# Block attention with a residual layer norm: softmax weights moved into the values' copy, the last row in halves, and a new order

## The chip, the cores and the metric

The kernel runs on one NeuronCore of a Trainium2 chip. Such a core has five engines with queues of their own: TensorE (PE in the profile, with its weight loads as PEld), VectorE (DVE), ScalarE (ACT), GpSimd (POOL) and SyncE (SP), which here only issues transfers. The metric is the device time of one execution in microseconds. Before the change it is 143.77 us, the median of three runs (143.69, 143.77, 144.44).

## The reference, cut to what matters

The input `x` is [8, 512, 1024] in float32. Each of the 8 batches is cut into 8 blocks of 64 rows, which are summed; the block sums are projected to keys, normalized, scored against one query, and a softmax over the 8 blocks weights the block sums. The weighted sum is projected by `Wo` to one vector for the batch, which is added to every row; the rows are then layer-normalized and added to `x`:

```python
block_repr = inputs.reshape(B, n_blocks, block_size, H).sum(axis=2)
keys = jnp.einsum('bnh,kh->bnk', block_repr, Wk)
keys = keys / rms * rms_weight
attn = jax.nn.softmax(jnp.einsum('bnh,h->bn', keys, q), axis=-1)
attended = jnp.einsum('bn,bnh->bh', attn, block_repr)      # the same for all rows of a batch
x = inputs + jnp.einsum('bsh,kh->bsk', attended, Wo)
out = (x - mu) / jnp.sqrt(var + EPS) * ln_gamma + ln_beta
return inputs + out                                        # 8 x 512 x 1024
```

The kernel uses that with y = inputs + proj the result is y * (1 + gamma * rs) + (beta - proj - mean * gamma * rs), where rs is one over the deviation: one multiplication of the row by a vector, and one addition of a vector, both different for every row.

## The kernel before, in words

The 4096 rows of `x` are worked in four groups of two batches (`GROUPS`). A group is 4 tiles `x_0` to `x_3` of 128 partitions with two rows each, so 8 rows of 1024 elements on every partition, and 32 such rows, k = 0 to 31, in all. Two successive rows are a unit (`UNITS`), 16 in all.

Before the first group both weight matrices are loaded, transposed on TensorE (L427) and copied to `wkT` and `woT` (L434), by VectorE for the copies in `EV_DVE` and else by ScalarE. The first 7 loads are three tiles of `Wk` and the four tiles of group 0; then come the last of `Wk`, `Wo`, and the `x` tiles of the other groups. There are 13 tile buffers (`XBUFS`), so later tiles wait for a weight tile to be transposed or for a store.

Each group goes through these steps:

- TensorE sums the blocks, `bs` (L592, four tiles); VectorE transposes the sums, `blkT` (L605); TensorE projects the keys (L460; L485 in group 0).
- ScalarE and VectorE take the squares and the product with the query (L624, L628); TensorE spreads them to all partitions, `pc` (L637, L640); ScalarE and VectorE make the scores and the softmax (L644 to L669). The result is `own`, one weight for each partition, where a partition stands for one block and one quarter of the columns.
- TensorE projects the values (L460, 32 steps of four narrow matmuls), ScalarE copies them to `val` (L700). Two selection matrices are scaled by `own` on ScalarE: `w` (L675) and `pickw` (L679).
- TensorE spreads the projected vector to all partitions, `pb` (L706), from `val` and `w`. It also makes the table `ptab` (L713, L714) from `val` and `pickw`, and from the matrix `gb`, which holds gamma and beta, with `pickv`. ScalarE copies it to `tab` (L718). The table holds, for each batch, the vectors that `b` needs.

Each row then goes through these:

- y (L759): VectorE adds `pb` to the row and sums it.
- Squares (L767): ScalarE takes the sum of the squared deviations, `ssq`.
- For a unit: GpSimd adds epsilon to `ssq` (L812), raises it to the power -0.5, `rs` (L813), and writes the row's factors to `stat` (L817, L822). TensorE transposes them, `pl` (L827), and ScalarE (for the units in `LT_ACT`) or VectorE copies them, `lt` (L834).
- Multiplication: for 26 rows ScalarE makes 1 + gamma * rs, `A` (L861), and GpSimd multiplies the row by it, called v here (L866). For the 6 rows in `ON_DVE` and `ON_BOTH` TensorE makes the factor in PSUM, `pA` (L872, L851), and VectorE multiplies (L878).
- Addition: TensorE makes the vectors to be added of both rows of the unit, `b` (L895), and VectorE adds them (L908), called out here. Then SP stores the tile (L915), the rows of the last two tiles one by one (L921).

The buffers that couple these steps are few. The two rows' banks of `b` are one pair, so the next `b` starts when both additions of the unit before are done. `stat` is one tile. `A` has three buffers, `lt` two. The bank `s2` is shared by values, `ptab` and `pl`.

The order of all this is written out. Every step is registered with `plan.add(engine, cost, emit, needs, ...)` and gets a number; `ORDER` lists the numbers in the order in which the instructions are emitted, and so fixes the order on each engine's queue. `FILLS` puts filler matmuls (`e_fill`, L952) ahead of a step: products of the identity with `gam` into a part of a bank that nobody reads. A filler leaves two records of 0.38 us that overlap; four fillers in a row took 1.89 us together.

Of the kernel before, what the change touches and what calls it, by code (L numbers as in the profile page):

```python
# [37 lines left out]
LT_ACT = (2, 3, 4, 5, 6, 7, 8, 9, 10, 11, 12, 13, 14, 15)  # L38
# [8 lines left out]
EV_DVE = (2, 3, 6, 9, 12, 15)  # L47
Y_PARTS = ()
EARLY_SUMS = 2
ROW_STORES = 2  # L50
ORDER = (
    0, 12, 1, 5, 6, 2, 3, 4, 7, 8, 9, 11, 10, 22, 24, 13, 63, 14, 25, 15, 26, 30, 27, 16, 23, 32,
    31, 55, 54, 28, 33, 17, 64, 29, 18, 57, 56, 65, 19, 20, 21, 66, 67, 70, 86, 34, 71, 68, 35, 36,
    69, 37, 58, 40, 38, 72, 73, 39, 42, 74, 41, 44, 75, 43, 76, 87, 48, 78, 77, 88, 46, 45, 79, 47,
    60, 59, 89, 49, 80, 81, 50, 90, 61, 52, 82, 51, 83, 91, 85, 53, 84, 95, 92, 93, 96, 94, 97, 98,
    173, 103, 99, 105, 104, 107, 106, 109, 174, 101, 102, 100, 119, 108, 175, 111, 120, 121, 125,
    176, 122, 113, 123, 110, 126, 127, 177, 115, 178, 179, 114, 117, 133, 180, 134, 129, 124, 135,
    181, 139, 137, 136, 191, 183, 182, 140, 128, 118, 184, 192, 130, 185, 131, 62, 116, 141, 186,
    138, 193, 187, 112, 194, 188, 143, 160, 142, 189, 267, 195, 147, 166, 198, 144, 145, 161, 190,
    162, 199, 268, 163, 148, 164, 167, 201, 149, 269, 150, 200, 203, 151, 165, 202, 205, 270, 146,  # L60
    204, 152, 153, 132, 196, 215, 206, 216, 271, 221, 154, 228, 207, 197, 222, 272, 155, 232, 273,
    156, 219, 234, 217, 274, 229, 233, 209, 157, 158, 168, 218, 211, 208, 230, 275, 170, 235, 231,
    285, 276, 169, 210, 286, 277, 213, 171, 220, 172, 223, 212, 159, 278, 225, 214, 287, 241, 224,
    279, 288, 254, 245, 280, 226, 227, 236, 242, 289, 246, 281, 243, 282, 237, 361, 283, 247, 255,
    292, 238, 258, 248, 362, 293, 239, 240, 260, 363, 295, 244, 294, 259, 364, 297, 249, 296, 365,
    299, 366, 298, 309, 256, 261, 367, 257, 300, 250, 251, 368, 313, 369, 301, 252, 253, 310, 322,
# [95 lines left out]
def block_attn_resid_kernel(  # L162
# [14 lines left out]
    HALF = 512  # L177
    QU = H // 4
    RT = 2
    UNIT = 4  # L180
    FAR = 1e30
    RS = float(H) ** 1.5
    assert RS == 2.0**15
# [267 lines left out]
    def project(rank, lhs, wT, tag, name, needs, hold, end, takes=None, parts=4):  # L451

        i = None
        for c0 in range(0, HC, HC // parts):
            def emit(c0=c0):
                if c0 == 0:
                    hold["po"] = half_bank(tag, name)
# [529 lines left out]
```

## Time and profile before

| | us |
|---|---|
| median of three runs | 143.77 |
| the profiled execution, whole | 144.35 |
| its span, first to last instruction | 142.6 |
| TensorE busy | 123.2 |
| VectorE busy | 100.0 |
| ScalarE busy | 95.2 |
| GpSimd busy | 84.2 |
| mean granted TensorE clock | 0.922 of full speed |

The profiled execution took 0.58 us more than the median, and 1.75 us of it lie outside the span. Durations below are from this one execution. The duration of an instruction is longer than the distance to the next on the same engine, because instructions overlap: y lasts 1.21 us, and the next starts 1.14 us after it. The distance is what counts on a full queue. The slices of busy time have one digit for each fortieth of the span, 3.57 us, in tenths. Where a row ends in brackets, the engine stood idle before it for that time, and the name is what it had waited for.

The stages show in the rows of instructions: the first y starts at 45.29 us, that of group 1 at 65.11, of group 2 at 88.21 and of group 3 at 109.74. The last addition on VectorE ends at 138.87.

### The profile page before, as it was taken

The page shows a single profiled execution, that of the slowest core. Times are in us where ns is not written, and L with a number is a line of the kernel's source. Part 1 is how long each engine was busy: PE and PEld are TensorE (multiplying, and loading weights), DVE is VectorE, ACT ScalarE, POOL GpSimd, SP SyncE. Part 2 cuts the span into 40 slices and gives each one's busy share as a digit, 9 for nine tenths or more (in the row PEclk, how much of TensorE's full clock was granted, in tenths as well). Part 3 has the DMA queues.
Part 4 walks back from the last instruction along what each step waited for, and adds up shares of the span by engine and source line. Part 5 has one row for each costly group of instructions (what it writes and reads, how often), then busy time and mean ns, then how long its engine had stood idle before and what let it go on. Part 6 is the DMA issues. An engine that isn't in the chain of part 4 may idle for free.

```text
span 142.6 us, 3107 instructions
## 1 busy us (share of the span) xinstructions
PE 123.2 (86%) x1202; PEld 68.8 (48%) x1202; DVE 100.0 (70%) x172; ACT 95.2 (67%) x165; POOL 84.2 (59%) x103
## 2 busy tenths in 40 slices
PE   0398996999999999999999999999898597799940
PEld 0375952875875745544544545446344264233400
DVE  6203121331462998687999989999999999986790
ACT  0306521345761999989999888998997999946000
POOL 7200000000020159998999999999989999999700
PEclk9999999999999999999999999999999959855555
DMA  4999999999999980199985499907616606756285
GB/s 114 428 403 426 418 408 406 409 414 423 416 423 414 420 365 21 74 310 414 375 292 241 184 306 379 379 11 294 257 74 280 276 37 262 294 221 257 110 349 239
DMA packets 7118, 42.15 MB, mean 296 GB/s; under 512 B 688, under 2 KB 704, under 8 KB 3264
## 3 DMA queue, kind: packets, MB, share of 16 engines
q1 hardware_dynamic: 7072, 41.95, 73.7%
q8 instruction: 9, 0.15, 0.4%
q14 instruction: 5, 0.04, 0.1%
q10 hardware_dynamic: 32, 0.02, 0.0%
HBM read 25.18 MB, written 16.78 MB: 294 GB/s over the span
## 4 chain that ended last, share of the span: by engine, by line
PE 45%; DVE 17%; DMA 14%; POOL 7%; issue 7%; ACT 6%; DVEq 1%; ACTq 0%; POOLq 0%
DMA x<-in_x_dram 10%; DVE x L908 7%; PE pt L427 7%; DVE x L759 7%; PE b L895 7%; PE bs L592 6%; POOL x L866 5%; PE pA L872 5%; PE keys L460 4%; DMA gb<-n_L_cond_rms_weight_dram 4%; PE keys L485 3%; PE values L460 3%; PE values L485 3%; ACT sq L767 3%; PE pl L827 2%
## 5 line engine op out<-in xcount | busy, mean ns | idle before, releaser
L866 POOL TENSOR_TENSOR x<-x,A 128x1024 f32<-128x1024 f32 x26 | 61.4, 2380 | 2.0 <-ACT A L861 1.9
L759 DVE SCALAR_TENSOR_TENSOR x<-x,pb 128x1024 f32<-128x1024 f32 x32 | 37.6, 1213 | 3.9 <-PE pb L549 2.9
L767 ACT ACTIVATE sq<-x,ysum 128x1024 bf16<-128x1024 f32 x32 | 36.7, 1146 | 2.9 <-DVE x L759 2.4
L908 DVE TENSOR_TENSOR x<-x,b 128x1024 f32<-128x1024 f32 x32 | 37.7, 1216 | 1.2 <-PE b L895 0.8
L861 ACT ACTIVATE A<-gam,rs 128x1024 f32<-128x1024 f32 x26 | 29.0, 1143 | 0.9 <-POOL rs L813 0.9
L895 PE MATMUL b<-tab,lt 32*128 32x512 f32 x128 | 24.1, 724 | 1.8 <-DVE x L908 0.9
L427 PE MATMUL pt<-ident,w 128*128 128x128 f32 x128 | 18.4, 300 | 6.4 <-DMA w<-in_L_cond_Wk_dram 5.9
L525 POOL TENSOR_SCALAR pickw<-early,own 128x256 f32<-128x256 f32 x1 | 0.9, 942 | 36.3 <-DVE junk L669 36.3
L427 PEld LDWEIGHTS pt<-ident,w 128*128 128x128 f32 x128 | 16.5, 197 | 9.4 <-issue 7.9
L592 PE MATMUL bs<-x,blk 128*32 128x256 f32 x256 | 16.4, 383 | 0.8 <-DMA x<-in_x_dram 0.5
L895 PEld LDWEIGHTS b<-tab,lt 32*128 32x128 f32 x128 | 7.7, 206 | 9.4 <-issue 3.5
L813 POOL TENSOR_TENSOR rs<-ssq,power 128x2 f32<-128x2 f32 x16 | 11.3, 707 | 1.3
L460 PE MATMUL values<-woT,blkT 128*32 128x256 f32 x192 | 12.0, 382 | 0.0
L460 PE MATMUL keys<-wkT,blkT 128*32 128x256 f32 x192 | 11.8, 383 | 0.2 <-DVE blkT L605 0.2
L592 PEld LDWEIGHTS bs<-x,blk 128*32 128x32 f32 x256 | 7.2, 110 | 7.9 <-issue 2.5
L812 POOL TENSOR_SCALAR ssq<-ssq 128x2 f32<-128x2 f32 x16 | 3.6, 223 | 8.7 <-ACT sq L767 7.4
L460 PEld LDWEIGHTS values<-woT,blkT 128*32 128x32 f32 x192 | 5.6, 109 | 6.2 <-issue 2.3
L872 PE MATMUL pA<-tabf,lt 32*128 32x512 f32 x16 | 7.2, 988 | 1.6 <-DVE x L759 0.9
L878 DVE TENSOR_TENSOR x<-x,pA 128x1024 f32<-128x1024 f32 x6 | 7.2, 1218 | 1.7 <-PE pA L872 1.7
L460 PEld LDWEIGHTS keys<-wkT,blkT 128*32 128x32 f32 x192 | 5.5, 109 | 5.9 <-DVE blkT L605 2.5
L434 DVE COPY wkT<-pt 128x1024 f32<-128x1024 f32 x3 | 3.7, 1225 | 6.4 <-PE pt L427 6.4
L827 PEld LDWEIGHTS pl<-ident,stat 128*128 128x128 f32 x16 | 2.3, 144 | 10.8 <-POOL stat L817 4.2
(104 smaller groups left out, 140.3 us busy)
## 6 DMA issues: line engine op xcount, KB each, us to landing
x<-in_x_dram SPq DMA_DIRECT2D x16, 1024.0 KB, 17.2
out_dram<-x SPq DMA_DIRECT2D x14, 1024.0 KB, 4.5
w<-in_L_cond_Wk_dram SPq DMA_DIRECT2D x4, 1024.0 KB, 9.3
w<-in_L_cond_Wo_dram SPq DMA_DIRECT2D x4, 1024.0 KB, 21.2
out_dram<-x SPq DMA_DIRECT2D x4, 512.0 KB, 2.8
gb<-in_cond_dram ACTq DMA_DIRECT2D x1, 4.0 KB
gb<-n_L_cond_rms_weight_dram ACTq DMA_DIRECT2D x1, 4.0 KB
gb<-in_L_cond_ln_gamma_dram ACTq DMA_DIRECT2D x1, 4.0 KB
```

Of the source, the lines that this page charges most:

```text
L427: nc.tensor.transpose(pt[:, c, r * P : (r + 1) * P], stage[which, s][:, r, bass.ds(4 * h4 + c, P, step=HC)], ident)
L460: nc.tensor.matmul(hold["po"][32 * j : 32 * j + 32, :], lhs(c), wT[:, c, bass.ts(j, QU)], start=(c == 0), stop=(end and c == HC - 1),)
L485: nc.tensor.matmul(T["po"][32 * j : 32 * j + 32, :], columns(2 * j + c), wT[:, 2 * j + c, bass.ts(s, QU)], start=(c == 0), stop=(c == 1),)
L592: nc.tensor.matmul(T["bs"][32 * j : 32 * j + 32, :], blk[g], G["x"][t][:, r, bass.ts(j, QU)], start=(t == 0 and r == 0), stop=(t == G["til ...
L759: nc.vector.scalar_tensor_tensor(x_row(k), x_row(k), 1.0, G["pb"], ALU.mult, ALU.add, accum_out=U["sum"][:, i : i + 1])
L767: nc.scalar.activation(junk, x_row(k), AF.Square, bias=U["sum"][:, i : i + 1], scale=-float(H), accum_out=U["ssq"][:, i : i + 1],)
L813: nc.gpsimd.tensor_tensor(U["rs"][:, :N], ssq, power[:, :N], ALU.pow)
L861: nc.scalar.activation(U["A", k], gam, AF.Identity, bias=1.0, scale=U["rs"][:, k - k0 : k - k0 + 1])
L866: nc.gpsimd.tensor_tensor(x_row(k), x_row(k), U.pop(("A", k)), ALU.mult)
L872: nc.tensor.matmul(U["pA", k][:, i, :], U["lt"][lo : lo + 32, pair, :], tabf[lo : lo + 32, :], start=True, stop=True,)
L895: nc.tensor.matmul(U["b", pair][r][:, i, :], U["lt"][lo : lo + 32, pair, :], G["T"]["tab"][lo : lo + 32, :], start=True, stop=True,)
L908: nc.vector.tensor_tensor(x_row(k), x_row(k), flat(U["b", pair][k % RT]), ALU.add)
```

## The change

- `own` becomes the scale of the activation that copies the values to `val`, in groups 1 to 3. `w` and `pickw` are not made any more; the unscaled matrices `weigh` and `pick` take their places. `val` now needs `own`.
- Gamma and beta get into `val` itself: a matmul `last2` by `gb` opens the accumulation of the values and puts them in the last two rows of each quarter, `own4` makes `own` 1 there, and `pick` gets their factors. So `ptab` has two matmuls in place of four. `own4`, `last2` and the entries of `pick` are made in the setup.
- Adding epsilon is a step of its own, on ScalarE for the five units in `EPS_ACT` and on GpSimd for the others.
- Row 31, the last, is added in two halves of 512 columns, each with a store of its own.
- `ORDER` is new from the start, and so is `FILLS`: 26 fillers at 10 places instead of 5 at 2. `LT_ACT` gets unit 0, and `EV_DVE` is another choice of seven copies instead of six.
- `UNIT` is 2 instead of 4, so `stat`, `lt` and `power` are smaller, and the pool of unit sums has 8 buffers instead of 16. The lines on `Y_PARTS` change too, but `Y_PARTS` is empty and they emit nothing.

In the new order, around the places that the prediction speaks of: all four `bs` of group 1 come ahead of `ptab` of group 0. The second `b` of group 0 follows all of group 1's values instead of the first half, with one filler after it and before `pb`. On VectorE the last additions of group 0 (tile 1) still come between the softmax and the first y of group 1. On GpSimd the multiplications of the last tile of group 0 change places. In the tail the fillers stand, in this order: one before `pb` of group 3, 5 before the second `pl` after it, 8 before `ptab`, 1 before the next `pl`, 5 before unit 12's `b`, 1 before the `pA` of row 26 and 2 before that of row 28. VectorE has the same rows in the same order in the tail, and the halves of row 31 come before row 30, which is whole. On ScalarE the epsilon of unit 13 comes after the copy of the last table. SP issues 21 loads before the first store; before it were 20.

```diff
-LT_ACT = (2, 3, 4, 5, 6, 7, 8, 9, 10, 11, 12, 13, 14, 15)
+LT_ACT = (0, 2, 3, 4, 5, 6, 7, 8, 9, 10, 11, 12, 13, 14, 15)
-EV_DVE = (2, 3, 6, 9, 12, 15)
+EV_DVE = (3, 6, 7, 9, 12, 13, 14)
+EPS_ACT = (6, 7, 11, 12, 13)
...
-FILLS = {343: 1, 411: 4}
+FILLS = {200: 1, 278: 1, 292: 1, 358: 5, 390: 8, 392: 1, 412: 1, 418: 5, 428: 1, 442: 2}
...
-    UNIT = 4
+    UNIT = max(UNITS)
...
-    unit = ctx.enter_context(tc.tile_pool(name="unit", bufs=len(UNITS)))
+    unit = ctx.enter_context(tc.tile_pool(name="unit", bufs=8))
...
+        for k in range(2):
+            for row, fill in ((GAM, -RS / H), (BET, 1.0)):
+                spots(fields(pick[g], k)[:, :, :, row : row + 1], [[0, 2], [-64, 2], [0, 1]], -32 * k - row, fill)
...
+    own4 = const.tile([P, 32], F32, tag="own4", name="own4")
+    nc.vector.tensor_scalar(own4, diag4, diag4[:, GAM : GAM + 1], diag4[:, BET : BET + 1], ALU.add, ALU.add)
+    last2 = const.tile([P, P], F32, tag="last2", name="last2")
+    nc.gpsimd.memset(last2, 0.0)
+    for k in (GAM, BET):
+        nc.vector.tensor_copy(
+            last2.rearrange("p (j m) -> p j m", m=32)[:, :, k : k + 1], by[:, :, k : k + 1]
+        )
...
-                junk3, T["pc"][:, 2, :NB], T["es"], diag4[:, :NB], ALU.mult, ALU.mult, accum_out=T["own"]
+                T["pc"][:, 3, :NB], T["pc"][:, 2, :NB], T["es"], own4[:, :NB], ALU.mult, ALU.mult, accum_out=T["own"]
...
-        def e_w():
-            T["w"] = chain.tile([P, 2, P], F32, tag="w", name=f"w{n}")
-            nc.scalar.activation(flat(T["w"]), flat(weigh[g]), AF.Identity, scale=T["own"])
-
-        def e_pick():
-            T["pick"] = chain.tile([P, 2, P], F32, tag="pickw", name=f"pickw{n}")
-            nc.scalar.activation(flat(T["pick"]), flat(pick[g]), AF.Identity, scale=T["own"])
...
+        def e_vectors(po):
+
+            nc.tensor.matmul(po, last2, gb, start=True, stop=False)
...
-            nc.scalar.copy(T["val"], T["values"]["po"])
+            nc.scalar.activation(T["val"], T["values"]["po"], AF.Identity, scale=T["own"])
...
-                nc.tensor.matmul(pb[:, j, :], T["w"][v, j % 2, :], T["val"][v, :], start=True, stop=True)
+                nc.tensor.matmul(pb[:, j, :], weigh[g][v, j % 2, :], T["val"][v, :], start=True, stop=True)
...
-                nc.tensor.matmul(T["ptab"][:, k, :], T["pick"][:, k, :], T["val"], start=True, stop=False)
-                nc.tensor.matmul(T["ptab"][:, k, :], pickv[:, k, :], gb, start=False, stop=True)
+                nc.tensor.matmul(T["ptab"][:, k, :], pick[g][:, k, :], T["val"], start=True, stop=True)
...
+        def e_eps():
+
+            ssq = U["ssq"][:, :N]
+            if u in EPS_ACT:
+                nc.scalar.activation(ssq, ssq, AF.Identity, bias=epsh_t)
+            else:
+                nc.gpsimd.tensor_scalar(ssq, ssq, EPS * H**3, None, ALU.add)
...
-            nc.gpsimd.tensor_scalar(ssq, ssq, EPS * H**3, None, ALU.add)
...
+                if k == NR - 1:
+
+                    for h in range(2):
+                        def e_half(k=k, out=e_out, h=h):
+                            out(k, (NR - 1 - k0) // RT, h * HALF, h * HALF + HALF)
+
+                        halves_.append(plan.add(DVE, 0.6, e_half, [bi, v], k + R["out"]))
+                    outs.append(halves_[-1])
+                else:
+                    outs.append(plan.add(DVE, 1.14, e_out, [bi, v], k + R["out"]))
...
+                    if k == NR - 1:
+                        for h, o in enumerate(halves_):
+                            stores.append(plan.add(SP, 0.35, lambda h=h: e_store_half(h), [o], k, moved=0.25))
+                    else:
+                        stores.append(plan.add(SP, 0.35, e_store_row, [o], k, moved=0.5))
```

## The prediction

> **What bounds the kernel now.** I read the page first: the span and the slices of busy time, then the costliest groups.
>
> ```profile
> span 142.6 us, 3107 instructions
> DVE  6203121331462998687999989999999999986790
> POOL 7200000000020159998999999999989999999700
> PEclk9999999999999999999999999999999959855555
> L866 POOL TENSOR_TENSOR x<-x,A 128x1024 f32<-128x1024 f32 x26 | 61.4, 2380 | 2.0 <-ACT A L861 1.9
> L759 DVE SCALAR_TENSOR_TENSOR x<-x,pb 128x1024 f32<-128x1024 f32 x32 | 37.6, 1213 | 3.9 <-PE pb L549 2.9
> L908 DVE TENSOR_TENSOR x<-x,b 128x1024 f32<-128x1024 f32 x32 | 37.7, 1216 | 1.2 <-PE b L895 0.8
> ```
>
> From about 45 us on VectorE is full, from 56 us GpSimd too; the average shares (70%, 59%) hide that. The TensorE clock falls to half in the last fifth. To see when, the table by stretches (us, busy of PE, PEld, DVE, ACT, POOL, then granted clock, DMA):
>
> ```profile
> 112.00:114.00 2.00, 1.00 (x6) 0.56 (x3) 2.00 (x5) 2.00 (x5) 1.90 (x2) 0.90 0.51 209
> 114.00:116.00 2.00, 2.00 (x6) 1.55 (x6) 2.00 (x4) 1.94 (x5) 2.00 (x2) 0.50 0.00 0
> 116.00:118.00 2.00, 2.00 (x12) 0.87 (x10) 2.00 (x4) 1.81 (x3) 1.83 (x3) 0.75 0.31 131
> 122.00:124.00 2.00, 1.12 (x11) 0.52 (x5) 2.00 (x5) 2.00 (x5) 2.00 (x2) 0.96 1.01 422
> 124.00:126.00 2.00, 2.00 (x8) 0.88 (x8) 2.00 (x3) 2.00 (x4) 1.75 (x6) 0.50 0.25 102
> ```
>
> Half clock from 113.6 to 117.0 and from 123.8 to the end. What it costs is VectorE's timeline in the tail (start, duration, what it did, idle before):
>
> ```profile
> 125.67 1.21 DVE L878 TENSOR_TENSOR x<-x,pA 128x1024 f32<-128x1024 f32 x1
> 127.29 2.35 DVE L908 TENSOR_TENSOR x<-x,b 128x1024 f32<-128x1024 f32 x2 [0.41 <-PE b L895]
> 130.84 1.22 DVE L878 TENSOR_TENSOR x<-x,pA 128x1024 f32<-128x1024 f32 x1 [1.19 <-PE pA L872]
> 132.47 2.35 DVE L908 TENSOR_TENSOR x<-x,b 128x1024 f32<-128x1024 f32 x2 [0.41 <-PE b L895]
> 135.38 1.22 DVE L878 TENSOR_TENSOR x<-x,pA 128x1024 f32<-128x1024 f32 x1 [0.56 <-PE pA L872]
> 136.52 2.35 DVE L908 TENSOR_TENSOR x<-x,b 128x1024 f32<-128x1024 f32 x2
> ```
>
> Waits of 0.41 + 1.19 + 0.41 + 0.56 = 2.57 us, all on slow matmuls. VectorE ends at 138.87; the last store needs 3.73 more. GpSimd's last multiply ends at 134.46, so it is about 3 us from binding. Earlier, one place matters, where group 0 hands over to group 1 (TensorE, then VectorE):
>
> ```profile
> 60.13 1.14 PE L895 MATMUL b<-tab,lt 32*128 32x512 f32 x8
> 61.20 1.93 PE L460 MATMUL values<-woT,blkT 128*32 128x256 f32 x32
> 61.83 2.35 DVE L908 TENSOR_TENSOR x<-x,b 128x1024 f32<-128x1024 f32 x2
> 65.11 1.22 DVE L759 SCALAR_TENSOR_TENSOR x<-x,pb 128x1024 f32<-128x1024 f32 x1 [0.93 <-PE pb L706]
> ```
>
> TensorE works without a break from 45.2 to 65.1, and VectorE adds rows from b meanwhile.
>
> [...] here L644 (16 elements, one pointer) took 0.266.
>
> **The change, part by part**, durations from the rows of before.
>
> Scalings gone: w and pickw, 2 x 3 x 0.50 = 3.0 us of ScalarE. They do not set pb: in group 1 w ends at 62.97 and val starts at 63.20; in group 2 row sums hold TensorE until 87.03, 0.5 after w; in group 3 values end after w. The new wait of val on own queues squares and A behind it; own comes at 61.97, 85.97, 106.2, before or about when values end. [...] I take 0 (from -0.5 to +0.3).
>
> Gamma and beta: two matmuls of 0.43 fewer per ptab, one of 0.43 more per values. In groups 1 and 2 that is -0.43 each; the last ptab, 3.6 us at half clock, becomes 0.86 at full. It gates only a table needed 4 us later: 0 by itself.
>
> Epsilon on ScalarE for 5 units: GpSimd gives up 5 x 0.31 (start of L812 to start of L813) = 1.55; ScalarE takes 5 x 0.2 (an estimate from L644 less overlap), in the room of the 3.0. No trace row has this form: gain between 0 and 1.55. In unit 13 it queues behind the copy of the last table, and GpSimd's next power waits: I charge 0.2.
>
> Setup: four selects of 0.21 and two fills on GpSimd, three small operations on VectorE. Hidden: GpSimd is idle till 40.8, VectorE from 4.7 to 11.9. Unhidden it would be 1.5. The first y at 45.29 hangs on the 7th load (22.1) and an unbroken 23 us of TensorE; the 7th load is an x tile still, and the same transposes follow: 0 (+-0.3).
>
> Moved with it: one more weight copy on VectorE (1.22) and one less on ScalarE (1.02), under TensorE's 23 us; unit 0's lt from VectorE (0.2) to ScalarE (0.15); half as many buffers for the units' sums, whose last readers are eight units back; on SP the 21st load goes ahead of the first store, and the last x load still goes behind stores of group 0 (80.8, its row sums at 88 to 91, DMA about 60% busy there). All 0; a load 3 us later would stop the row sums.
>
> Halves: row 31 is added in halves, but the order puts row 30, whole, after it. So the last store stays 512 KB behind a whole addition. 128x512 has no row; between L628 (0.42 at 256) and L908 (1.22 at 1024) a half takes about 0.69, two cost 0.1 more. One more store is issued (0.33 on SP, before the last addition ends). +0.1 (from -0.3 to +0.4).
>
> The order, group 0 to 1: the second b now stands behind all of values, and one filler stands before pb. Also all four row sums come ahead of ptab, so the transpose waits about 0.5 for them. From 45.2: sums 4.0, ptab 2.8, keys 4.0, two pl 0.5, b 1.07, pc 0.8, last2 0.43, values 4.0: b starts at 62.8, ends 63.9. VectorE, through with own at 62.0, waits for it, adds two rows to 66.2 and only then starts y: 66.2 against 65.11, so **+1.05**. GpSimd is free at 66.0, but the A it takes first stands on ScalarE behind an lt, which needs the pl after pb: 67.1; twice more it waits for squares of later rows (0.6, 0.8). That is 2.4 us of gaps where before had 0.5, and the 1.55 saved pay back most of it later. Groups 1 and 2: the same rows on VectorE (65.11 to 88.21 is 23.1, 0.5 of it idle). TensorE has five row sums 5.0, keys 4.0, values with last2 4.4, four b 4.3, a pair of pA 1.1, ptab 0.9, four pl 1.0, pc 0.8, pb 1.1, two fillers 0.9: 23.5, just as full. So nothing is caught up, and I carry the 1.05 on. y of group 3 then starts at 110.8 against 109.74.
>
> The tail: the same rows on VectorE in the same order. Fillers: 5 + 8 + 1 + 5 + 1 + 2 = 22 x 0.43 (1.89 for four, less the overlap) = 9.5 us against 5 x 0.43. The stretches 110.2 to 123.8 then are over 90% busy and keep the clock. Then b (1.07) fits beside the multiplication by pA (1.13), and the **2.57 go**. What is late next: GpSimd, about 1 us later than before through the last group, makes two or three additions wait, in all 0.4 with the 0.2 above.
>
> Sum on VectorE's end: 138.87 + 1.05 + 0.1 - 2.57 + 0.4 = 137.85; plus 3.73: span 141.6 against 142.6. The profiled run took 144.35, 1.75 outside the span, and stands 0.58 above the median 143.77. With 1.75 the forecast is 143.35, by ratio to the median 142.8. I say **142.9**.
>
> **The rivals.**
> *One window lost and regained.* After 124 there are few fillers: a pA of 1.06, then about 1.1 us without work until b's bank is free. [...] Then one b, two fillers and a pA run late by 1.3 us. Span 142.9: 144.2.
> *Lost to the end* (the other side). As before, where a window full of pA and b at half clock from 123.8 did not bring it back. Two fillers then cost 1.7 us ahead of a pA, and pA with b takes 3.78 (128.64 to 132.42) in place of 2.1, in three units: VectorE ends about 3.9 later, at 141.8; span 145.5, run 146.8. It decides as soon as the clock drops before about 129.
> *GpSimd binds.* Its gaps in group 1 are larger than I walked them, or ScalarE's epsilon holds it up: 1.5 us more before it frees rows. For it: it is 95% full from 60 on. Against: 1.55 of its work is gone. Run 144.4.
> *No gain from the clock*, held but irrelevant: excluded by the idle lines above.
>
> **How the numbers follow.** The forecast 0.48 (own range 141.5 to 143.5; 0.40 of it faster, 0.08 same). One window lost 0.20 (0.12 same, 0.08 slower). Lost to the end 0.17, slower. GpSimd 0.15 (0.04 same, 0.11 slower). Faster by over 0.5% 0.40, within 0.5% 0.24, slower 0.36; 0.5% is about what a measurement of this kernel can tell from no change. A tenth lies below 140.8 (the order hides the 1.05 too); upward I go to 146.8, the case of the clock lost.
>
> **What would show it.** Right: half clock nowhere between 110 and 125; VectorE's idle from 124 on under 1 us; the first y of group 1 near 66.2 with VectorE idle before a b at 62 to 64; squares' epsilon on ScalarE near 0.2; the last store 3.7 us long. Wrong: fillers of 0.86 in the trace, a pA of 2 us, or additions waiting on GpSimd for over 2 us in all. [...]

## The result, and the profile after

| | before | after |
|---|---|---|
| median of four runs, us | 143.99 (143.69 to 144.44) | 145.48 (145.42 to 145.61) |
| profiled execution, whole | 144.35 | 145.45 |
| its span | 142.6 | 143.6 |
| first y of groups 0, 1, 2, 3 | 45.29, 65.11, 88.21, 109.74 | 45.65, 65.67, 90.02, 111.63 |
| end of VectorE's last addition | 138.87 | 139.65 |
| end of GpSimd's last multiply | 134.46 | 136.93 |

The ratio is 1.0098, with a 95% interval of 1.0069 to 1.0127: the kernel became 1% slower, where 142.9 had been forecast.

The page of the kernel after: span, slices of busy time, and the groups that answer to those shown of before.

```profile
span 143.6 us, 3196 instructions
DVE  6204001631762996849999898999999999999970
POOL 7500000000020169986869988999979997999910
PEclk9999999999999999999999999999999999999955
L884 POOL TENSOR_TENSOR x<-x,A 128x1024 f32<-128x1024 f32 x26 | 61.5, 2378 | 3.2 <-ACT A L879 3.1
L769 DVE SCALAR_TENSOR_TENSOR x<-x,pb 128x1024 f32<-128x1024 f32 x32 | 37.6, 1214 | 3.1 <-PE pb L567 2.9
L927 DVE TENSOR_TENSOR x<-x,b 128x1024 f32<-128x1024 f32 (+1 forms) x33 | 38.0, 1183 | 5.0 <-PE b L913 4.4
```

The clock row has lost its fives but for the last two. In exchange VectorE waits 5.0 us ahead of its additions, where before it was 1.2, and GpSimd 3.2 ahead of its multiplies instead of 2.0. The stretches (us, busy of PE, PEld, DVE, ACT, POOL, then clock, DMA) confirm the clock:

```profile
112.00:114.00 2.00, 2.00 (x11) 1.56 (x9) 2.00 (x5) 2.00 (x4) 2.00 (x3) 1.00 0.95 393
116.00:118.00 2.00, 2.00 (x11) 1.77 (x10) 2.00 (x4) 1.69 (x5) 2.00 (x2) 1.00 0.01 4
124.00:126.00 2.00, 1.66 (x11) 0.50 (x11) 2.00 (x5) 1.97 (x3) 2.00 (x2) 1.00 0.96 393
136.00:138.00 2.00, 1.19 (x4) 0.00 (x0) 1.43 (x3) 0.00 (x0) 0.93 (x1) 0.52 0.82 326
```

It is full to 136, where 0.50 stood before. VectorE's timeline in the tail:

```profile
127.79 1.21 DVE L896 TENSOR_TENSOR x<-x,pA 128x1024 f32<-128x1024 f32 x1
129.11 1.22 DVE L927 TENSOR_TENSOR x<-x,b 128x1024 f32<-128x1024 f32 x1
130.48 1.22 DVE L927 TENSOR_TENSOR x<-x,b 128x1024 f32<-128x1024 f32 x1
131.62 1.22 DVE L896 TENSOR_TENSOR x<-x,pA 128x1024 f32<-128x1024 f32 x1
137.23 2.42 DVE L927 TENSOR_TENSOR x<-x,b 128x512 f32<-128x512 f32 x3 [0.57 <-PE b L913]
```

The waits of 0.41, 1.19, 0.41 and 0.56 for slow matmuls are gone; 0.57 remains, for the last b, after the clock fell at 136 (its second half takes 1.61 us, from 135.58). The shorter waits between the rows, as the 1.37 from 129.11 to 130.48 in place of 1.14, are for GpSimd, whose multiplication ended at 130.44. So the tail gave about half of what it was to give: from the first y of group 3 to the last addition it takes 28.02 us, against 29.13 before and 27.05 in the forecast. The kernel is slower because group 3 starts 1.89 us later. Of that, 0.36 is there at the first y, 0.20 comes by group 1, 1.25 in group 1 itself (from 65.67 to 90.02), and 0.08 in group 2. TensorE's timeline around the places:

```profile
62.12 1.14 PE L913 MATMUL b<-tab,lt 32*128 32x512 f32 x8
63.19 0.70 PE L992 MATMUL pc<-gam,ident 128*128 128x256 f32 x2
63.82 1.14 PE L717 MATMUL pb<-val,weigh 64*128 64x256 f32 x8
...
73.00 0.70 PE L992 MATMUL bs<-gam,ident 128*128 128x256 f32 x2 [0.32 <-DVE blkT L623]
73.75 1.07 PE L478 MATMUL keys<-wkT,blkT 128*32 128x256 f32 x16
...
84.84 0.70 PE L992 MATMUL pc<-gam,ident 128*128 128x256 f32 x2 [0.21 <-ACT pc L679]
85.47 1.07 PE L478 MATMUL values<-woT,blkT 128*32 128x256 f32 x16
```

And VectorE's first y of group 2:

```profile
90.02 1.21 DVE L769 SCALAR_TENSOR_TENSOR x<-x,pb 128x1024 f32<-128x1024 f32 x1
```

L992 is a filler. Start to start, one alone takes 0.63 to 0.75 us here, not 0.43. And a filler can wait: it writes into an unread part of a bank, and the bank has other users. At 73.00 it waits 0.32 for the transposition of the row sums, as the keys behind it would (0.37 in the run without it, below), so it cannot fill that hole; at 84.84 it waits 0.21 for the softmax.

### The profile page after: what moved, and what is told of

Its sections match the earlier page's. It is cut to its first block, busy times and chain, and to the rows that moved or that the text cites. A ratio compares the mean times of both kernels' runs of the same rounds, so it can differ in the third digit from the quotient of the medians.

```text
span 143.6 us, 3196 instructions
## 1 busy us (share of the span) xinstructions
PE 126.2 (88%) x1238; PEld 71.1 (49%) x1238; DVE 101.3 (71%) x176; ACT 93.4 (65%) x164; POOL 83.7 (58%) x104
## 4 chain that ended last, share of the span: by engine, by line
PE 54%; DMA 14%; POOL 14%; DVE 8%; issue 3%; ACT 3%; DVEq 0%; POOLq 0%; ACTq 0%
DMA x<-in_x_dram 10%; POOL x L884 10%; PE b L913 8%; PE pt L443 7%; PE values L478 7%; PE keys L478 6%; PE pc L992 5%; PE bs L610 4%; DMA gb<-n_L_cond_rms_weight_dram 4%; DVE x L927 3%; PE keys L503 3%; PE values L503 3%; DVE x L769 2%; POOL rs L830 2%; DVE x L896 2%
## 5 line engine op out<-in xcount | busy, mean ns | idle before, releaser
L927 DVE TENSOR_TENSOR x<-x,b 128x1024 f32<-128x1024 f32 (+1 forms) x33 | 38.0, 1183 | 5.0 <-PE b L913 4.4
L913 PE MATMUL b<-tab,lt 32*128 32x512 f32 x128 | 21.1, 644 | 0.5 <-DVE x L927 0.2
L992 PE MATMUL pc<-gam,ident 128*128 128x256 f32 x50 | 12.7, 390 | 0.2 <-ACT pc L679 0.2
L992 PEld LDWEIGHTS pc<-gam,ident 128*128 128x128 f32 x50 | 8.9, 193 | 4.3 <-issue 2.7
L913 PEld LDWEIGHTS b<-tab,lt 32*128 32x128 f32 x128 | 6.0, 183 | 7.6 <-issue 3.1
L623 DVE STREAM_TRANSPOSE blkT<-bs 128x256 f32<-128x256 f32 x4 | 1.8, 447 | 9.8 <-PE bs L610 9.7
L824 POOL TENSOR_SCALAR ssq<-ssq 128x2 f32<-128x2 f32 x11 | 2.4, 221 | 10.0 <-ACT sq L777 9.4
L851 ACT COPY lt<-pl 128x128 f32<-128x128 f32 x15 | 3.8, 256 | 5.3 <-PE pl L844 5.2
```

What stands on the lines that cost most here:

```text
L913: nc.tensor.matmul(U["b", pair][r][:, i, :], U["lt"][lo : lo + 32, pair, :], G["T"]["tab"][lo : lo + 32, :], start=True, stop=True,)
L927: nc.vector.tensor_tensor(x_row(k)[:, c], x_row(k)[:, c], flat(U["b", pair][k % RT])[:, c], ALU.add)
L992: nc.tensor.matmul(at, ident, gam[:, :QU], start=True, stop=True)
```

## The experiments

Four theories (the first three are theories 1 to 3 of the expectations). **T1, fillers**: the four single fillers ahead of the tail are paid on TensorE's full queue. **T2, order**: the new order costs (the second b behind the values, GpSimd's gaps). **T3, parts**: val behind own, last2, and the detour of epsilon cost. **T4, clock**: the tail's fillers are worth the 2.5 us that VectorE waited. All runs, with the ratio to the kernel before on the same chip. They are from four chips, on which the medians of the kernel before lie between 143.74 and 144.00, so a difference of 0.3 us between two medians from different chips shows nothing; where a part is priced below, the marks of the profiled executions stand beside it.

| kernel | median, us | ratio, 95% interval |
|---|---|---|
| after without its four early fillers | 143.86 | 1.0009 (0.9992 to 1.0026) |
| after without any filler | 145.98 | 1.0152 (1.0126 to 1.0178) |
| all parts, old order | 146.65 | 1.0196 (1.0157 to 1.0234) |
| before, tail filled | 142.55 | 0.9914 (0.9888 to 0.9941) |
| before, tail filled, weight in val's copy only | 143.55 | 0.9970 (0.9955 to 0.9985) |
| before, tail filled, gamma and beta in the rows only | 144.21 | 1.0032 (1.0008 to 1.0055) |
| new order, old parts | 145.22 | 1.0078 (1.0050 to 1.0106) |
| all parts, old order, tail filled | 145.20 | 1.0098 (1.0055 to 1.0140) |
| after without early fillers, epsilon on GpSimd | 144.89 | 1.0070 (1.0041 to 1.0098) |
| weight in val's copy, a row sum ahead of pl | 143.02 | 0.9940 (0.9921 to 0.9960) |
| the same, five epsilons on ScalarE | 144.15 | 1.0019 (1.0008 to 1.0031) |
| before, tail filled, two early fillers | 143.66 | 0.9987 (0.9967 to 1.0008) |
| before, tail filled, row sum behind pb | 143.13 | 0.9947 (0.9928 to 0.9966) |
| after without early fillers, 3 before the table | 142.95 | 0.9942 (0.9919 to 0.9965) |

### The fillers taken away, early ones and all

```diff
-FILLS = {200: 1, 278: 1, 292: 1, 358: 5, 390: 8, 392: 1, 412: 1, 418: 5, 428: 1, 442: 2}
+FILLS = {358: 5, 390: 8, 412: 1, 418: 5, 428: 1, 442: 2}
```

> The kernel after without its four single fillers ahead of the tail (before pb of group 1, before the first quarter of group 2's keys, before the last quarter of group 2's values, before pb of group 3). Theory 1, the fillers are what the chain on TensorE pays: each stood in it for 0.63 to 0.75 us, so y of group 1 comes about 0.6 earlier (65.0), y of group 2 about 1.8 (88.2), y of group 3 about 1.8 to 2.4 (109.3 to 109.8); span 141.5 to 142.3, time 143.3 to 144.2. Theory 2, the order costs (second b of group 0 behind the values, row sums ahead of the table, gaps on GpSimd): y of group 3 comes less than 0.5 earlier and the time stays within 0.4 of the kernel after, 145.1 to 145.5.

Measured: 143.86, within what T1 gives, though only the two fillers of group 2 turn out to cost anything. The first y of the groups comes at 45.74, 65.76, 88.63 and 110.54. The filler of group 1 had cost nothing (65.67 with it, 65.76 without): VectorE was still adding its two rows while it ran. That of group 3 was covered too: without it pb waits 0.59 for val, at 109.36. The two of group 2 cost 1.39 between them (90.02 to 88.63), about what their records add up to: 0.75 + 0.63 + 0.21 of waiting, less 0.17 that a b waits when they are gone. TensorE's timeline without them:

```profile
73.09 1.07 PE L478 MATMUL keys<-wkT,blkT 128*32 128x256 f32 x16 [0.37 <-DVE blkT L623]
...
82.12 2.80 PE L478 MATMUL values<-woT,blkT 128*32 128x256 f32 x48
85.09 1.14 PE L913 MATMUL b<-tab,lt 32*128 32x512 f32 x8 [0.17 <-DVE es L684]
```

```profile
88.63 1.21 DVE L769 SCALAR_TENSOR_TENSOR x<-x,pb 128x1024 f32<-128x1024 f32 x1
```

The keys wait 0.37 for the transposition and start at 73.09; with the filler, at 73.75. Of the 1.6 us, 1.09 are there at y of group 3; the tail takes 27.56 in place of 28.02, because its last b still comes at full clock (1.00 from 134 to 136).

```diff
-FILLS = {200: 1, 278: 1, 292: 1, 358: 5, 390: 8, 392: 1, 412: 1, 418: 5, 428: 1, 442: 2}
+FILLS = {}
```

> The kernel after without any filler. If the tail's fillers are what holds the clock, it falls to half at about 112 to 114 and again near 124, VectorE's waits for pA and b from 124 on come back to about 2.5 us, and the time is 144.0 to 145.0 if the early fillers cost about 1.8 (theory 1), 146.5 to 147.5 if they cost nothing (theory 2). If the tail's fillers hold nothing, full clock stays to 136 and the time is 143 or less.

Measured: 145.98, so the tail's fillers are worth 2.12 us (145.98 against 143.86). The clock falls, as the stretches show, and from 127 on VectorE waits 0.48, 0.43, 0.60, 0.41, 0.55 and 0.42, in all 2.9:

```profile
112.00:114.00 2.00, 2.00 (x9) 0.49 (x6) 2.00 (x5) 2.00 (x5) 2.00 (x2) 0.50 0.65 262
118.00:120.00 2.00, 0.90 (x3) 0.18 (x1) 2.00 (x5) 1.87 (x4) 1.84 (x6) 0.61 0.00 0
128.00:130.00 2.00, 1.64 (x7) 0.69 (x5) 1.57 (x3) 0.50 (x2) 1.75 (x6) 0.50 1.05 438
```

The time lies between the two expectations (144.0 to 145.0, and 146.5 up). The early fillers explain 1.6 us, but this kernel without any filler is 2.2 slower than the one before, so more is lost than fillers.

### The kernel before, with its tail filled

```diff
-FILLS = {343: 1, 411: 4}
+FILLS = {343: 2, 384: 2, 411: 5, 420: 2, 424: 2, 437: 1, 451: 1}
```

> The kernel before, with fillers in its tail alone: 14 in place of 5, set before b of unit 10, the last table, b of units 12 to 15 and pA of row 26. If the half clock in the tail costs what VectorE's waits of 2.57 us show, the clock is full from 110 to 136, the waits from 124 on fall below 0.8 and the time is 141.3 to 142.5. If GpSimd or something else takes over as the bound, the clock is full and the time stays within 0.7 of the kernel before. If the fillers don't hold the clock, they cost 0.86 each and the time is 144.5 or more.

Measured: 142.55, 0.86% faster than before and 1.8% faster by ratio than after: the best of all runs. Marks up to group 3 are those of before (109.75), the clock is full past 136 (1.00 in every stretch from 108), no wait for a slow matmul is left in VectorE's timeline, and it ends at 136.85, 2.02 earlier than in the profiled execution of before. So T4 has the cause right, but not its size: 2.02, not 2.5. What is late next is GpSimd (GpSimd's timeline, then VectorE's):

```profile
129.79 4.68 POOL L866 TENSOR_TENSOR x<-x,A 128x1024 f32<-128x1024 f32 x2
```

```profile
129.50 1.22 DVE L878 TENSOR_TENSOR x<-x,pA 128x1024 f32<-128x1024 f32 x1
133.32 1.21 DVE L878 TENSOR_TENSOR x<-x,pA 128x1024 f32<-128x1024 f32 x1
134.50 2.35 DVE L908 TENSOR_TENSOR x<-x,b 128x1024 f32<-128x1024 f32 x2
```

GpSimd works with no break over 0.1 us from 124.59 to the end of its last multiplication at 134.47, and the last additions start at 134.50. VectorE's units follow each other at GpSimd's 3.82 us (129.50 to 133.32), where three of its own distances of 1.14 are 3.42. The kernel has 15 fillers (not 14, as the expectation counts): ten more than before, in places where TensorE has room, are worth 1.2 us without any of the parts.

### Parts and order: a square

The parts in the old order: each step of the kernel after was put where the old order has the same step; val took the place of w, and epsilon went right before the power.

```diff
-LT_ACT = (0, 2, 3, 4, 5, 6, 7, 8, 9, 10, 11, 12, 13, 14, 15)
+LT_ACT = (2, 3, 4, 5, 6, 7, 8, 9, 10, 11, 12, 13, 14, 15)
-EV_DVE = (3, 6, 7, 9, 12, 13, 14)
+EV_DVE = (2, 3, 6, 9, 12, 15)
-EPS_ACT = (6, 7, 11, 12, 13)
+EPS_ACT = ()
...
-FILLS = {200: 1, 278: 1, 292: 1, 358: 5, 390: 8, 392: 1, 412: 1, 418: 5, 428: 1, 442: 2}
+FILLS = {350: 1, 418: 4}
```

> All parts of the change in the code, but in the order of the kernel before, with its fillers, its choice of copies and epsilon left on GpSimd; row 31's halves stand where its whole addition stood. If the order and the fillers are what costs (theories 1 and 2), the time is that of the kernel before or a little less: 143.5 to 144.1. If the parts cost (theory 3: val behind own on ScalarE, last2 of 0.5 to 0.6 on the chain of each group), y of groups 1 to 3 comes 0.5, 1.0 and 1.5 later than before, and the time is 145 or more.

The same with its tail filled:

```diff
-FILLS = {350: 1, 418: 4}
+FILLS = {350: 2, 390: 2, 418: 5, 428: 2, 432: 2, 446: 1, 461: 1}
```

> All parts of the change in the old order as in the run before (146.65), but with the tail's fillers of the filled kernel before. The clock there fell already at 103 us, behind a stall. If most of its loss was clock, the time falls by 2 us or more, to 143.5 to 144.6; if it was the waits for val and last2 that the parts make in the old order, it falls by less than 1 us, to 145.6 to 146.5, with y of group 2 still near 90.2.

And the kernel before in the new order, with the new choices of copies:

```diff
-LT_ACT = (2, 3, 4, 5, 6, 7, 8, 9, 10, 11, 12, 13, 14, 15)
+LT_ACT = (0, 2, 3, 4, 5, 6, 7, 8, 9, 10, 11, 12, 13, 14, 15)
-EV_DVE = (2, 3, 6, 9, 12, 15)
+EV_DVE = (3, 6, 7, 9, 12, 13, 14)
...
-FILLS = {343: 1, 411: 4}
+FILLS = {350: 5, 384: 8, 405: 1, 411: 5, 420: 1, 433: 2}
```

> The new order with the old parts (w and pickw on ScalarE, w behind own, pickw behind pb; unscaled val; four matmuls for a table; epsilon on GpSimd beside the power; row 31 whole), with the tail's fillers of the kernel after but none of the four early ones. With the runs before it closes a square of old and new order by old and new parts. If the new order is made for the new parts, it gains nothing without them: 144 to 145, worse than the kernel after without early fillers (143.86). If the order is good by itself and the parts cost in any order, 142.5 to 143.4.

With the kernel just shown and the one without early fillers they make a square; all four have their tails filled and no early fillers.

| medians, us | old parts | new parts |
|---|---|---|
| old order | 142.55 | 145.20 |
| new order | 145.22 | 143.86 |

Without the filled tail the parts in the old order took 146.65; filling it gained 1.45, between the two expectations, and y of group 2 stays at 90.2. So T2 and T3 are both right, and neither alone: the parts cost 2.65 in the old order, the new order costs 2.67 with the old parts (2.4 by the ratios), and together they cost 1.31. The new order repairs much of what the parts break, and costs by itself where they are not there. Two things are mixed in: only the kernel at the lower right has epsilon on ScalarE for five units, and with it back on GpSimd, as in the other three, it takes 144.89 (below); and the lower row has 22 fillers, 8 of them before the last table, where the upper has 15 at other places. With epsilon alike the two together cost 2.34, still well under the sum of 5.32.

### Which part costs in the old order

```diff
-            nc.scalar.copy(T["val"], T["values"]["po"])
+            nc.scalar.activation(T["val"], T["values"]["po"], AF.Identity, scale=T["own"])
...
-                nc.tensor.matmul(pb[:, j, :], T["w"][v, j % 2, :], T["val"][v, :], start=True, stop=True)
+                nc.tensor.matmul(pb[:, j, :], weigh[g][v, j % 2, :], T["val"][v, :], start=True, stop=True)
...
-                nc.tensor.matmul(T["ptab"][:, k, :], T["pick"][:, k, :], T["val"], start=True, stop=False)
+                nc.tensor.matmul(T["ptab"][:, k, :], pick[g][:, k, :], T["val"], start=True, stop=False)
```

> The kernel before with its tail filled (as in the run before), and of the change only the weight as the scale of the values' copy (and row 31 in halves); gamma and beta still come by matmuls into the table, and the order is the old one, val where w stood. Theory: what the parts cost in the old order is val waiting for own while it keeps the bank s2, which the next pl needs. Then val of group 2 starts near 87 in place of 84.9, a pl waits over 1 us for it, y of group 2 starts 1.0 to 1.5 later than 88.24 and the time is 143.5 to 145. Rival: the matmul last2 on TensorE's full queue is what costs; then this kernel stays within 0.4 of the one before with its tail filled, 142.3 to 142.9.

Measured: 143.55, 1.0 more than without. Up to group 1 little changes (y at 65.28 against 65.14, as the first y is 0.15 later); y of group 2 starts at 89.24 in place of 88.24, so group 1 takes 23.96 in place of 23.10. TensorE's timeline, and ScalarE's:

```profile
84.39 1.14 PE L914 MATMUL b<-tab,lt 32*128 32x512 f32 x8
86.83 0.30 PE L845 MATMUL pl<-ident,stat 128*128 128x128 f32 x1 [1.31 <-ACT val L711]
87.06 1.07 PE L610 MATMUL bs<-x,blk 128*32 128x256 f32 x16
88.06 1.13 PE L717 MATMUL pb<-val,weigh 64*128 64x256 f32 x8
```

```profile
86.21 0.47 ACT L711 ACTIVATE val<-values,own 128x256 f32<-128x256 f32 x1 [0.63 <-DVE pc L686]
```

ScalarE's in the kernel before with its tail filled:

```profile
84.92 0.35 ACT L700 COPY val<-values 128x256 f32<-128x256 f32 x1
```

There val was copied out of the bank s2 from 84.92, as soon as ScalarE came to it. Now it waits for own until 86.21, and pl, which needs the same bank, stands first in TensorE's queue for 1.31 us, with the row sum and pb behind it. This kernel has row 31 in halves too; from y of group 3 to the end it takes 27.04, the one without them 27.10, so the halves cost nothing there.

To tell the bank from a late val, one step was moved: the row sum that stood behind pl now stands ahead of it.

```diff
-    216, 291, 245, 246, 227, 285, 292, 259, 260, 250, 286, 229, 230, 240, 247, 251, 287, 248, 288,
-    241, 369, 293, 252, 261, 296, 242, 264, 253, 370, 297, 243, 244, 266, 371, 299, 249, 298, 265,
+    216, 291, 245, 246, 227, 285, 292, 259, 260, 250, 286, 229, 230, 240, 247, 251, 287, 288, 241,
+    369, 248, 293, 252, 261, 296, 242, 264, 253, 370, 297, 243, 244, 266, 371, 299, 249, 298, 265,
```

> The old order with the weight in the values' copy alone (143.55), with one step moved: in group 2 the first row sum of group 3 now stands ahead of the pl that waited 1.31 us for val. Theory, bank s2 is kept until val has read it, and what costs is that pl stands first in TensorE's queue: the row sum fills the hole, pl and pb follow at 87.1 and 87.4, y of group 2 starts at 88.4 to 88.5 in place of 89.24, the time is 142.6 to 143.1. Rival, val itself is late and pb with it: pb stays near 88, y at 89.2, the time at 143.4 to 143.7.

Measured: 143.02, and y of group 2 at 88.52. TensorE's timeline:

```profile
86.08 1.07 PE L610 MATMUL bs<-x,blk 128*32 128x256 f32 x16 [0.69 <-PE b L914]
87.08 0.33 PE L845 MATMUL pl<-ident,stat 128*128 128x128 f32 x1
87.34 1.13 PE L717 MATMUL pb<-val,weigh 64*128 64x256 f32 x8
```

The row sum runs where TensorE stood still, and group 1 takes 23.37: 0.59 of the 0.86 come back, and 0.53 of the 1.0 in the time. So half or more of the part's cost is what stands behind pl while val holds the bank; the rest was not taken apart.

Gamma and beta alone, with w and pickw as before:

```diff
+            nc.tensor.matmul(po, last2, gb, start=True, stop=False)
...
-                nc.tensor.matmul(T["ptab"][:, k, :], T["pick"][:, k, :], T["val"], start=True, stop=False)
-                nc.tensor.matmul(T["ptab"][:, k, :], pickv[:, k, :], gb, start=False, stop=True)
+                nc.tensor.matmul(T["ptab"][:, k, :], T["pick"][:, k, :], T["val"], start=True, stop=True)
```

> The kernel before with its tail filled, and of the change only gamma and beta in the values' last rows (last2, and two matmuls for a table in place of four); w and pickw are still scaled and val is copied as soon as the values end. Theory val behind own: this costs nothing or gains a little, 142.0 to 142.8. Rival, last2: in groups 1 to 3 b and pc come 0.5 to 0.6 later each time, VectorE waits about 0.6 for the second b of group 2, and the time is 143.2 to 144.2.

Measured: 144.21, 1.66 more, at the upper end of what the rival, last2, gives. The profiled execution took 145.46, since the clock fell in it at 102.7 (0.68 from 102 to 104, then 0.50); only what comes before that is read. VectorE's and TensorE's timelines:

```profile
82.61 2.35 DVE L925 TENSOR_TENSOR x<-x,b 128x1024 f32<-128x1024 f32 x2 [0.59 <-PE b L912]
```

```profile
98.33 1.13 PE L731 MATMUL ptab<-val,pickw 128*128 128x256 f32 x4
99.30 0.53 PE L651 MATMUL pc<-diag,sd 128*128 128x32 f32 x4
99.66 0.39 PE L654 MATMUL pc<-apart,ident 128*128 128x32 f32 x2
101.32 0.30 PE L844 MATMUL pl<-ident,stat 128*128 128x128 f32 x1 [1.27 <-ACT tab L735]
```

The last of these rows in the kernel before with its tail filled:

```profile
100.48 0.30 PE L827 MATMUL pl<-ident,stat 128*128 128x128 f32 x1 [0.41 <-ACT tab L718]
```

Two matmuls fewer per table do not come out as time: the next pl needs the table's bank and waits 1.27 for ScalarE's copy of it, where before it waited 0.41. The one matmul more, though, stands ahead of values, pc and b, and VectorE waits 0.59 for the b behind it. What was saved lies where TensorE waits anyway, what was added where it does not. And in this execution the clock fell 1.4 us after that hole, with TensorE busy for 2.13 of the 3.41 us before (62%); four of the 20 executions took 145.4 or more.

### Epsilon

```diff
-EPS_ACT = (6, 7, 11, 12, 13)
+EPS_ACT = ()
...
```

(The lines of `ORDER` are left out.) In the new order, without early fillers, epsilon of every unit back on GpSimd, ahead of the power:

> The kernel after without its early fillers (143.86), with epsilon of all units back on GpSimd, just ahead of the power. The prediction's step: the five moved epsilons save GpSimd 1.55 and cost 0.2 in unit 13. If that holds and GpSimd is near the bound, its last multiply ends later than 135.85 by up to 1.3 and the time is 144.3 to 145.0, near the old parts in the new order (145.22). If the detour over ScalarE takes as much as it saves (waits of 0.3 to 0.5 for a squares' epsilon), the time stays at 143.6 to 144.1.

Measured: 144.89, so five epsilons on ScalarE gain 1.0 there (0.9 by the ratios). Without them y of group 3 comes at 111.13 instead of 110.54 (VectorE waits 0.66 for a b at 103.74), and the end is 1.0 later. This also sets the rest of the square: 145.22 with old parts against 144.89 leaves a gain of 0.33 for the weight, the rows and the halves together, too little to tell from none (1.0078 and 1.0070 by the ratios). In the old order the same five were moved to ScalarE, on top of the row sum ahead of pl:

```diff
-EPS_ACT = ()
+EPS_ACT = (6, 7, 11, 12, 13)
```

> The old order with the weight in the values' copy and the row sum ahead of pl (143.02), now with the epsilon of units 6, 7, 11, 12 and 13 on ScalarE. If GpSimd's 1.55 us are worth 1.0 wherever they are saved, as in the new order, the time is 141.9 to 142.4. If GpSimd isn't what sets the end in the old order (VectorE waits for it nowhere from 65 us on), the gain is 0, and the added hops can only cost: 142.9 to 143.5.

Measured: 144.15, 1.13 slower. GpSimd's timeline:

```profile
83.52 1.34 POOL L831 TENSOR_TENSOR rs<-ssq,power 128x2 f32<-128x2 f32 x2 [0.70 <-ACT ssq L823]
118.10 0.69 POOL L831 TENSOR_TENSOR rs<-ssq,power 128x2 f32<-128x2 f32 x1 [0.69 <-ACT ssq L823]
120.24 0.69 POOL L831 TENSOR_TENSOR rs<-ssq,power 128x2 f32<-128x2 f32 x1 [1.16 <-ACT ssq L823]
```

Here the powers stand where they stood, and wait 0.7 to 1.2 us each for an addition queued on ScalarE. VectorE then waits 0.80 for a multiply at 126.03. The expectation had GpSimd off the bound in the old order; yet in both kernels the last additions start as its last multiplication ends (134.75 after 134.72, and 135.99 after 135.96). So GpSimd sets the end there, and the moved step cost it more in waits than it saved. The same edit gains 1.0 or loses 1.1 by its place in two queues.

### Two fillers more, a row sum moved, and the fillers before the table

```diff
-FILLS = {343: 2, 384: 2, 411: 5, 420: 2, 424: 2, 437: 1, 451: 1}
+FILLS = {343: 2, 384: 2, 411: 5, 420: 2, 424: 2, 437: 1, 451: 1, 272: 1, 288: 1}
```

> The kernel before with its tail filled (142.55), and two of the early fillers of the kernel after added at their places in group 2: ahead of the first quarter of the keys and ahead of the last quarter of the values. At the prediction's 0.43 each, y of group 2 comes at most 0.9 later (89.1) and the time is 143.2 to 143.5. At what the kernel after shows, 1.39 for the two, y of group 2 starts at 89.4 to 89.6 and the time is 143.6 to 144.0. If VectorE has slack there, y moves by less than 0.4.

Measured: 143.66, 1.11 more; y of group 2 at 89.38, 1.14 later. Group 1 takes 24.09 in place of 23.10; in the new order the two fillers made it 24.35 in place of 22.87. So two fillers on a full queue cost 1.0 to 1.5 in either order.

```diff
-    138, 193, 187, 112, 194, 188, 143, 160, 142, 189, 267, 195, 147, 166, 198, 144, 145, 161, 190,
+    138, 193, 187, 112, 194, 188, 143, 160, 142, 189, 195, 147, 166, 198, 267, 144, 145, 161, 190,
```

> The kernel before with its tail filled (142.55), and the first row sum of group 2 moved from ahead of pb of group 1 to behind it. TensorE then waits for val and not for the sum: pb at 63.6 in place of 63.95, y of group 1 at 64.8. If VectorE sets the end from there, all marks come 0.35 earlier and the time is 142.1 to 142.4; if the sum is missed later, y of group 2 is back at 88.2 and the time stays at 142.4 to 142.7.

Measured: 143.13, a miss on the other side. y of group 1 comes 0.42 earlier (64.72), as thought, and that of group 2 0.40 later (88.64). TensorE now stands still for 0.49 ahead of pb; its next table starts 0.49 later (70.20 against 69.71), own 0.40 later. On this full TensorE the hole is lost for good, although y of group 1 gained by it at once.

```diff
-FILLS = {358: 5, 390: 8, 412: 1, 418: 5, 428: 1, 442: 2}
+FILLS = {358: 5, 390: 3, 412: 1, 418: 5, 428: 1, 442: 2}
```

> The kernel after without its early fillers (143.86), and with 3 in place of 8 fillers ahead of the last table. Theory: the 8 fillers put the table 3.7 us back, its copy stands ahead of an epsilon on ScalarE, and GpSimd waits 0.47 and 0.36 for that; with 3 the table comes 2.1 us earlier, the two waits shrink below 0.2 each, GpSimd's last multiply ends 0.5 earlier (135.3) and the time is 143.2 to 143.6. Rival: the wait is epsilon's own way over ScalarE and back; then the waits stay and so does the time, 143.6 to 144.1. If 3 do not keep the clock, half clock shows near 117 to 121 and the time is 144.3 or more.

Measured: 142.95, 0.9 less than with 8, and below the 143.2 to 143.6 of the theory. What the 8 did shows in the kernel after, on TensorE, ScalarE and GpSimd:

```profile
115.11 3.72 PE L992 MATMUL pc<-gam,ident 128*128 128x256 f32 x16
118.67 1.03 PE L724 MATMUL ptab<-val,pick 128*128 128x256 f32 x4
```

```profile
119.73 0.58 ACT L728 COPY tab<-ptab 128x512 f32<-128x512 f32 x1 [0.66 <-PE ptab L724]
120.22 0.30 ACT L822 ACTIVATE ssq<-ssq,epsh_t 128x2 f32<-128x2 f32 x1
```

```profile
120.59 0.69 POOL L830 TENSOR_TENSOR rs<-ssq,power 128x2 f32<-128x2 f32 x1 [0.47 <-ACT ssq L822]
121.64 0.21 POOL L834 TENSOR_TENSOR stat<-ysum,rs 128x4 f32<-128x4 f32 x1 [0.36 <-POOL rs L830]
```

The table stands 3.7 us behind fillers, its copy waits for it 0.66 with an epsilon behind, and GpSimd loses 0.83. The chain of work that ended last goes the same way: fillers, table, b, and then GpSimd, which works from 121.6 to 134.3 with no break over 0.1 us. With 3, neither wait is left. The profiled execution with 3, though, took 144.63, 1.7 over the median: its clock fell at 127.6 (0.90 from 126 to 128, then 0.50), where with 8 it held to 136 (1.00), and VectorE waited 1.48 for a pA. Two more of the 20 executions took 144.4 to 144.5. That the 5 left out would have held it in these was not shown.

## Why the prediction was wrong

Two steps failed: the price of single fillers in group 1, where 0 was carried on and 1.25 us came; and the tail, where GpSimd was taken to be 3 us from binding and the step behind the fillers was charged 0.2. The profiled execution was to take 143.35 and took 145.45. Of these 2.1 us, 0.83 are there at y of group 3 (111.63 against 110.8), 0.97 come in the tail, 0.22 in the last store (3.95 us against 3.73), and 0.10 outside the span. By its own steps:

- **The tail keeps its clock**: right, full to 136 (1.00 in every stretch from 110, and 110.2 to 123.8 is 99% busy, 13.47 of 13.60 us). By the kernel without fillers this is worth 2.12 us.
- **"The 2.57 go", and GpSimd "about 3 us from binding"**: this step failed. With the same waits gone in the old order, the tail takes 27.10 against 29.13, 2.03 less, because GpSimd then sets VectorE's pace: the last additions start at 134.50, as its last multiplication ends at 134.47.
- **What stands behind the fillers of the tail**: named (unit 13 behind the table's copy), but charged 0.2. GpSimd lost 0.83 there, and the run with 3 fillers gains 0.9. The tail takes 28.02, where the sum had 27.05; 0.57 of that is the wait for the last b, after the clock fell at 136, and the 0.5 us too many of the line above is in it too.
- **Group 0 to 1, +1.05**: the shape was right, down to VectorE's wait before a b at 63.40. The walk was a microsecond too long: that b started at 62.12, not 62.8, and y at 65.67, not 66.2; 0.36 of the +0.56 was there at the first y.
- **"23.5, just as full. So nothing is caught up, and I carry the 1.05 on"**: this step failed. 23.5 is 0.4 more than the 23.1 of before, and the two fillers in it were priced as in a row (0.43), not as single ones on a full queue (0.75 and 0.63, and 0.21 of waiting). Group 1 took 24.35, and 22.87 without them, less than the 23.10 of before: so the fillers are the whole of the 1.25. A size was off, and the sum was not read for what it said.
- **First y, 0 (+-0.3)**: +0.36. It comes on TensorE, where the same matmuls stand in another order: the last ones of the keys start at 34.07 before and at 34.08 after, the last ones of pb at 43.69 and 44.05. In the kernels of the new order it comes at 45.50 to 45.84, in those of the old at 45.07 to 45.47.
- **The parts at 0 by themselves**: wrong in the old order (1.0 for the weight, 1.66 for the rows), about right in the new (a gain of 0.33 with the halves, not clear of the noise). "I take 0" looked at when own comes, not at who waits for the bank that val holds. For the rows the step summed matmuls and didn't ask where each stood.
- **Epsilon**: 1.55 less 0.2 forecast as GpSimd's gain, 1.0 measured in the time, in the new order. Halves: 0.1 forecast, nothing seen.
- **The profiled execution**: before's stood 0.58 over its median, and the forecast took that off. After's (145.45) stood at its median (145.48). That is about 0.5 of the miss of 2.6 in the median.
- **Busy share and clock**: in the kernel before, the 3.40 us ahead of the two falls of the clock (as long as its half-clock stretch, 113.6 to 117.0) were 47% and 48% busy (1.59 from 110.2, 1.63 from 120.4), and 3.40 us that kept it, from 21.4, were 66% busy (2.25). That a limit lies between was the author's estimate, and it is not borne out. Just before the clock fell TensorE was 82% busy in the kernel after (2.80 of 3.40, to 136.1) and 62% with gamma and beta in the rows (2.13 of 3.41, to 102.7); and in the kernel before, 3.40 us of TensorE without a break from 123.8, at half clock (0.50), were followed by half clock to the end. So the busy share of these stretches doesn't tell by itself when the clock falls; what does stays open.

The rival "GpSimd binds" was right for the tail (its epsilons are worth 1.0, and the chain that ended last runs along GpSimd there); in group 1 the bound that moved was TensorE's queue. The two clock rivals did not come true.

Not settled: why the new order with the new parts, without early fillers, stays 1.3 behind the old order with old parts. 3 fillers before the table leave 0.4 of the 1.3, and its first y is 0.5 late (45.84 against 45.32); whether that is the same time was not tried.

## What to carry to other kernels

The tail's fillers held the clock here (1.00 in place of 0.50, worth 2.12 us); such fillers belong where the engine has holes, and each place has its own price: here nothing where something else is late anyway, 0.63 to 0.75 us where the queue is full, and 0.21 more at 84.84, where the filler waited for another user of its bank. A step moved behind a later value keeps its buffer until then (val started at 86.21 in place of 84.92, and pl waited 1.31 for the bank), so ask who is next in line for the buffer and what stands behind that one. Parts of a change and an order found for them are judged together: each alone cost about 2.7 us here, both together 1.3 (2.3 with epsilon alike), and the gain that was had (1.2 us) needed neither. And before a wait is counted as gain, look who is next: of 2.57 us of waits 2.03 came back, up to where GpSimd stood.

## What the runs showed of the hardware

A matmul of 128x128 by 256 columns in float32 takes 0.43 to 0.45 us in a row of its like (`ptab` in the kernel before with its tail filled, from 98.03 to 98.46 and 98.89; 8 fillers in 3.56, from 115.11 to 118.67, in the kernel after), but 0.63 to 0.75 alone between others (63.19 to 63.82, and 73.00 to 73.75, in the kernel after). The same kernel loses the clock before its end in some executions and, by their times, not in others: with gamma and beta in the rows 16 of the 20 executions took 143.87 to 144.66 at a mean granted clock of 0.974 to 0.985, and four took 145.46 to 145.69 at 0.964 to 0.972; the profiled one of these (145.46) lost it at 102.7; with 3 fillers before the table 16 executions took 142.56 to 143.09 at a mean granted clock of 0.982 to 0.992, and three took 144.40 to 144.63 at 0.970 to 0.971; the profiled one of these lost it at 127.6.
